# Inverse roots as a power on GpSimd, Silu and Sigmoid by way of Tanh, and one inversion of row sums as a power, in a four-layer image kernel

## The chip, the cores and the metric

The kernel runs on one core of one Trainium2 chip. The metric is the device time of one execution in microseconds (us), lower is better. A core has five engines with a queue each, worked off in order: TensorE (PE in the profile; its weight loads are PEld), VectorE (DVE), ScalarE (ACT), GpSimd (POOL) and SyncE (SP), which here issues the transfers.

## The reference

Eight images of 256 channels and 32 x 32 places, in fp32, go through four layers. Each layer is `x = x + layer(group_norm(x))`, with 32 groups of 8 channels.

```python
# layer 0: attention over the 1024 places, 8 heads of 64, q and k of length 1, scale 10
# layers 1 and 2: 3x3 convolutions, 256 to 256 channels
# layer 3:
xn = layernorm(xs, norm_w, norm_b)                    # over the 256 channels
xm = mamba_v(xc, ...) + skip_scale * xc               # 4 blocks of 64 channels
g  = jax.nn.sigmoid(Q)                                # Q: two small convolutions of xm
# gate, depthwise and 1x1 convolutions -> xm2
x_global = mha(xm2, ...)                              # 8 heads of 32, softmax over 1024 places
x_out = gelu(layernorm(concat([x_local, x_global]) @ fc_w.T + fc_b))
# normalize each channel over its places, 3x3 depthwise, layernorm, 1x1
def mamba(...):                                       # 128 inner channels, 16 states
    u  = silu(conv1d(u)); dt = softplus(...)
    y  = selective_scan(u, dt, B, C, A, D)            # h = exp(dt*A)*h + dt*u*B, over 1024 places
    return y * silu(z) @ outw.T
```

Four kinds of places in it matter here: the inverse square roots of the norms (group norm, layer norm, the length of q and k), the two `silu` of each Mamba block, the `sigmoid` of the gate, and the division by the softmax's row sums in the attention of layer 3.

## The kernel before

Channels lie on the 128 partitions, in two tiles, and places along the free dimension (N = 1024, halves of 512). One image at a time goes through `layer0`, `layer1`, `layer2` and `layer3`; the next image is loaded ahead. The code is written for a framework that sets the waits, and orders the instructions of each engine's queue by its own plan; the order is fixed when the program is built. Working tiles come from one pool of 20 buffers (`work`, tile tag `t`); PSUM has two `mm` tiles of 512 columns, two `big` and one `acc` of 1024.

- `rsqrt_of` (L135): VectorE adds eps (L137), ScalarE takes the square root (L138), VectorE the reciprocal (L139). `group_norm` calls it on a 128x2 tile, four times per image, and the channel norm near the end of layer 3 once. Whatever follows (L168) needs its result.
- `layer_norm` (L177), three times per image: means by a matmul (L185), squares, variances by a matmul (L196) into an 8x128 tile, then add (L204), square root (L205), reciprocal (L206), and a matmul that spreads the result over the partitions (L211).
- `rows_of` in `layer0` (L407): the sum of squares of each row of q and k, square root (L426), maximum with 1e-12 (L427), reciprocal (L428); then the row is scaled (L435, L436).
- `mamba` (L562), four blocks per image. A prologue: a projection, a convolution of four taps on VectorE (L588, L597), Silu on ScalarE (L600), a projection of u (L606) and of dt (L619), softplus from Abs, Exp and Ln (L622 to L629), the product of dt and u (L631). Then a loop over 16 states, with one state spread ahead: a row of B comes by DMA (L638), ScalarE makes exp(dt*A) (L641), TensorE spreads C (L646), GpSimd multiplies (L653), VectorE scans (L662) and multiplies by C (L663), TensorE adds up (L665). Last, u is joined (L672), Silu of z is made from PSUM (L676) and multiplied in on GpSimd (L677), and projected (L680, L683). In VectorE's queue the last seven of the 16 multiplies (L663) stand behind the last scan.
- The gate of layer 3: two matmuls per half (L802, L816), Sigmoid (L824), multiply (L826).
- `attention` (L334) of layer 3: for each pair of heads and half of the places eight units of scores (L344), Exp (L352) and values (L360). The values' matmul gives the row sums too, in the upper 32 rows; `take` copies values (VectorE, L762) and sums (ScalarE, L763) out of PSUM. Four heads fill one tile of sums, `rs[t]`. Then `note` finds its smallest and largest sum (L331, L332), L776 inverts, L777 multiplies, L778 adds a bias:

```python
        for t in range(2):
            r = rs[t][:, 0:N]
            note(r)
            nc.vector.reciprocal(r, r)
            nc.vector.tensor_mul(o[t][:, 0:N], o[t][:, 0:N], r)
```

In VectorE's queue the part for `t = 0` stands between the PSUM copies of the second and the third pair of heads, so in the middle of the attention.

The functions with `exact` belong to a second pass that is taken only if a row sum was out of bounds; with these inputs it isn't taken.

Of the kernel before, what the change touches and what calls it, by code (L numbers as in the profile page):

```python
# [10 lines left out]
F32 = mybir.dt.float32  # L11
# [17 lines left out]
def preact_stack(ctx: ExitStack, tc: tile.TileContext, I, out, cols):  # L29
# [38 lines left out]
    def col(name, i=0, rows=slice(0, P)):  # L68
        at = cols[name] + i
        return vec[rows, at : at + 1]  # L70
# [60 lines left out]
    a_neg = wp.tile([P, NB * DS], F32, name="a_neg")  # L131
    nc.scalar.activation(a_neg, vec[:, cols["alog"] : cols["alog"] + NB * DS], AF.Exp)
    nc.vector.tensor_scalar_mul(a_neg, a_neg, -1.0)

    def rsqrt_of(t, eps):  # L135

        nc.vector.tensor_scalar_add(t, t, eps)  # L137
        nc.scalar.activation(t, t, AF.Sqrt)  # L138
        nc.vector.reciprocal(t, t)  # L139

    def channel_stats(srcs):

# [34 lines left out]
    def layer_norm(srcs, dsts, finish):  # L177

        sq = []
        for t in range(2):  # L180
            sq.append(work("ln_sq"))
        for h in range(2):
            pm = mm_tile()
            for t in range(2):
                nc.tensor.matmul(  # L185
                    pm, mean_w, srcs[t][:, HALVES[h]], start=t == 0, stop=t == 1
                )
            for t in range(2):
                nc.vector.tensor_sub(dsts[t][:, HALVES[h]], srcs[t][:, HALVES[h]], pm)
                nc.scalar.activation(  # L190
                    sq[t][:, HALVES[h]], dsts[t][:, HALVES[h]], AF.Square
                )
        pv = mm_tile()
        for i in range(NKT):
            for t in range(2):
                nc.tensor.matmul(  # L196
                    pv[0:NKT, 0:P],
                    var_w[:, i],
                    sq[t][:, i * P : (i + 1) * P],
                    start=i == 0 and t == 0,  # L200
                    stop=i == NKT - 1 and t == 1,
                )
        rs = sp.tile([NKT, P], F32, tag="ln_rs", name="ln_rs")
        nc.vector.tensor_scalar_add(rs, pv[0:NKT, 0:P], 1e-5)  # L204
        nc.scalar.activation(rs, rs, AF.Sqrt)  # L205
        nc.vector.reciprocal(rs, rs)  # L206
        for h in range(2):
            pr = mm_tile()
            for i in range(4):
                blk = h * 4 + i  # L210
                nc.tensor.matmul(  # L211
                    pr[:, i * P : (i + 1) * P],
                    ident[0:NKT, blk : blk + 1].to_broadcast([NKT, P]),
                    rs,
                    start=True,
                    stop=True,
                )
            for t in range(2):
                part = dsts[t][:, HALVES[h]]
                nc.vector.tensor_mul(part, part, pr)  # L220
                finish(t, part)
# [167 lines left out]
    def layer0(xt, exact=False):  # L389
        xn = [work("xn0"), work("xn1")]  # L390
        group_norm(xt, [t[:, 0:N] for t in xn])

        v = vp.tile([P, NKT, 512], F32, tag="v", name="v")

        def values(kt):
            ps = mm_tile()
            for c in range(2):
                nc.tensor.matmul(
                    ps,
                    xn[c][:, kt * P : (kt + 1) * P],  # L400
                    wqkv[:, c, 1024:1536],
                    start=c == 0,
                    stop=c == 1,
                )
            nc.vector.tensor_copy(v[:, kt], ps)

        def rows_of(first, name):  # L407

            a = work(name)
            ss = sp.tile([P, 2], F32, tag="ss", name="ss", bufs=4)  # L410
            for h in range(2):
                ps = mm_tile()
                for c in range(2):
                    nc.tensor.matmul(  # L414
                        ps,
                        wqkv[:, c, first : first + P],
                        xn[c][:, HALVES[h]],
                        start=c == 0,
                        stop=c == 1,
                    )  # L420
                nc.vector.tensor_copy(a[:, HALVES[h]], ps)
            sq = work("sq")
            nc.scalar.activation(
                sq[:, 0:N], a[:, 0:N], AF.Square, accum_out=ss[:, 0:1]
            )
            nc.scalar.activation(ss[:, 1:2], ss[:, 0:1], AF.Sqrt)  # L426
            nc.vector.tensor_scalar_max(ss[:, 1:2], ss[:, 1:2], 1e-12)  # L427
            nc.vector.reciprocal(ss[:, 1:2], ss[:, 1:2])  # L428
            return a[:, 0:N], ss[:, 1:2]

        qs, ks = [], []
        for t in range(4):
            q, rq = rows_of(t * P, "q")
            k, rk = rows_of(512 + t * P, "k")
            nc.vector.tensor_scalar(q, q, rq, 10.0, ALU.mult, ALU.mult)  # L435
            nc.vector.tensor_scalar_mul(k, k, rk)  # L436
            qs.append(q)
            ks.append(k)
            for kt in (2 * t, 2 * t + 1):
                values(kt)  # L440

        o = []

        def heads():
            for t in range(4):
                o.append(work("o"))
                for e in range(2):
                    yield head(t, e)

        def head(t, e):  # L450
            rows = slice(e * 64, e * 64 + 64)
            at = t * P + e * 64

            def take(half, acc):
                nc.vector.tensor_copy(o[t][rows, half], acc)

            return {
                "q": qs[t][rows],
                "k": ks[t][rows],
                "v": lambda kt: v[:, kt, at : at + 64],  # L460
                "rows": rows,
                "take": take,
            }

        def pair(t):
            ot = work("o")
            o.append(ot)
            rows = [slice(e * 64, e * 64 + 64) for e in range(2)]

            def v_of(e):  # L470
                at = t * P + e * 64
                return lambda kt: v[:, kt, at : at + 64]

            def take(h, acc, total):
                ps = mm_tile()
                for e in range(2):
                    nc.tensor.matmul(
                        ps[rows[e]],
                        ones,
                        total[:, HALVES[e]],  # L480
                        start=True,
                        stop=True,
                    )
                rs = work("rs0")[:, 0:HALF]
                nc.scalar.copy(rs, ps)
                note(rs)
                nc.vector.reciprocal(rs, rs)
                nc.vector.tensor_mul(ot[:, HALVES[h]], acc, rs)

            return {  # L490
                "q": [qs[t][r] for r in rows],
                "k": [ks[t][r] for r in rows],
                "v": [v_of(e) for e in range(2)],
                "take": take,
            }

        if exact:
            attention_exact(heads())
        else:
            attention([pair(t) for t in range(4)], True)  # L500

        def evac(m, half, ps):
            nc.vector.scalar_tensor_tensor(
                xt[:, m, half], ps, col("b_out", m), xt[:, m, half], ALU.add, ALU.add
            )

        project(wout, o, evac)
# [54 lines left out]
    def mamba(i, xn, xm):  # L562
# [33 lines left out]
        for k in range(3):  # L596
            nc.vector.scalar_tensor_tensor(  # L597
                uu, raw[:, k : k + N], col("convw", 4 * i + k), uu, ALU.mult, ALU.add
            )
        nc.scalar.activation(uu, uu, AF.Silu)  # L600


        low = work("low")
# [69 lines left out]
            uu, uu, col("mD", i), y_acc, ALU.mult, ALU.add  # L673
        )
        z = work("z")
        in_proj(P, lambda h, ps: nc.scalar.activation(z[:, HALVES[h]], ps, AF.Silu))  # L676
        nc.gpsimd.tensor_mul(uu, uu, z[:, 0:N])  # L677
        for h in range(2):
            ps = mm_tile()
# [12 lines left out]
    def mixer_attention(x2, exact=False):  # L692
# [80 lines left out]
        for t in range(2):  # L773
            r = rs[t][:, 0:N]
            note(r)
            nc.vector.reciprocal(r, r)  # L776
            nc.vector.tensor_mul(o[t][:, 0:N], o[t][:, 0:N], r)  # L777
            nc.vector.tensor_scalar_add(o[t][:, 0:N], o[t][:, 0:N], col("ain_b", 4 + t))  # L778
        return o

    def layer3(xt, out_b, exact=False):
# [31 lines left out]
        for h in range(2):  # L813
            for j in range(2):
                ps = mm_tile()
                nc.tensor.matmul(  # L816
                    ps,
                    qpr[:, 2 * j : 2 * j + 2].rearrange("q b m -> q (b m)"),
                    q4[0:NB, HALVES[h]],
                    start=True,  # L820
                    stop=True,
                )
                gate = work("gate")[:, 0:HALF]
                nc.scalar.activation(gate, ps, AF.Sigmoid, bias=col("qpwb", j))  # L824
                part = inner(xm[j])[:, HALVES[h]]
                nc.vector.tensor_mul(part, part, gate)  # L826
        xg = xm
# [237 lines left out]
```

## Time and profile before

| | |
|---|---|
| Time, median of 2 runs | 9571.7 us (9569.48 to 9573.92) |
| The profiled execution: its time / its span | 9565.23 us / 9563.5 us |
| PE busy | 7354.8 us, 77% of the span |
| DVE busy | 5074.7 us, 53% |
| ACT busy | 2543.9 us, 27% |
| POOL busy | 2190.2 us, 23% |
| Mean granted TensorE clock | 0.862 |
| HBM read / written | 286.83 MB / 10.49 MB |

The span is the time from the first to the last instruction; the time is that of the whole execution. In the rows of instruction groups the columns are: source line, engine, operation, output<-input with partitions x elements, count, then busy us and mean ns of one, then the engine's idle time just before them and what ended it. In the timeline the columns are: start, length, engine, line, operation, tiles, count, and in brackets the idle time before it with what ended that. A line of the timeline can stand for several instructions in a row. `ACT_TABLE_LOAD` is ScalarE's change to another set of function tables.

### The profile page before, as it was taken

To read this page: it belongs to the slowest core of one execution; us is meant where nothing else is said; L and a number is where in the kernel's file an instruction comes from. 1 tells how busy PE (TensorE), PEld (TensorE's weight loads), DVE (VectorE), ACT (ScalarE), POOL (GpSimd) and SP (SyncE) were. 2 spreads that over 40 slices of the span, in tenths; PEclk is the share of its full clock that TensorE was granted. 3 is DMA by queue.
4 is the path that set the end of the run, shared out by engine and by line. 5 is a ranking of instruction groups with operands and counts; after the bars stand their busy time and mean duration, and the time that the engine had idled before them with its cause. 6 is when DMAs were issued, how large, how long until landed. Compare 5 with 4: busy or idle time off the path is not lost.

```text
span 9563.5 us, 51820 instructions
## 1 busy us (share of the span) xinstructions
PE 7354.8 (77%) x19650; PEld 2690.0 (28%) x19650; DVE 5074.7 (53%) x4146; ACT 2543.9 (27%) x2835; POOL 2190.2 (23%) x1021
## 2 busy tenths in 40 slices
PE   9767897678975789757897578976789757897577
PEld 2322233222332223322233222332223322233222
DVE  6466364663646636466364663646536465364653
ACT  3121331213312133121331213312133121331213
POOL 0253002530025300253002530025300252002520
PEclk9878998788987889878898788987889878898788
DMA  1111001110012100121001210012100121001210
GB/s 51 36 64 42 0 9 36 69 38 2 8 36 69 38 0 9 36 69 38 3 7 36 69 38 5 5 36 71 36 9 0 36 71 36 5 1 36 71 36 5
DMA packets 86139, 300.76 MB, mean 31 GB/s; under 512 B 9844, under 2 KB 12532, under 8 KB 85368
## 3 DMA queue, kind: packets, MB, share of 16 engines
q1 hardware_dynamic: 85880, 297.36, 9.1%
q8 instruction: 156, 2.56, 0.1%
q14 instruction: 103, 0.84, 0.0%
HBM read 286.83 MB, written 10.49 MB: 31 GB/s over the span
## 4 chain that ended last, share of the span: by engine, by line
PE 59%; DVE 23%; issue 9%; POOL 4%; ACT 4%; DMA 0%; DVEq 0%; POOLq 0%; ACTq 0%
PE mm L533 11%; PE mm L360 10%; DVE hs L662 10%; PE big L344 7%; PE acc L665 5%; PE mm L255 4%; PE big L646 4%; PE acc L344 4%; PE mm L414 3%; DVE hs L663 2%; POOL hs L653 2%; DVE u L597 1%; DVE dw L920 1%; PE mm L606 1%; PE mm L716 1%
## 5 line engine op out<-in xcount | busy, mean ns | idle before, releaser
L665 PE MATMUL acc<-hs,ident 128*128 128x512 f32 x2048 | 1211.6, 726 | 1257.2 <-DVE hs L663 1256.9
L653 POOL TENSOR_TENSOR hs<-a,hs 128x1024 f32<-128x1024 f32 x512 | 1887.5, 3715 | 250.5 <-DMA hs<-b_rows 230.2
L662 DVE TENSOR_TENSOR_SCAN hs<-da,hs 128x1024 f32<-128x1024 f32 x512 | 1826.0, 3598 | 219.6 <-POOL hs L653 204.4
L360 PE MATMUL mm<-p,v 128*64 128x512 f32 x4096 | 1098.0, 617 | 0.0
L646 PE MATMUL big<-u,w_mxpw 128*128 128x512 f32 x2048 | 1076.3, 655 | 0.0
L533 PE MATMUL mm<-im,w_wc 128*128 128x512 f32 x2304 | 1033.5, 612 | 29.2 <-DVE im L168 25.6
L641 ACT ACTIVATE da<-dt,a_neg 128x1024 f32<-128x1024 f32 x512 | 563.7, 1142 | 1648.0 <-DVE hs L662 1460.9
L352 ACT ACTIVATE p<-big 128x1024 f32<-128x1024 f32 x688 | 702.4, 1023 | 1014.4 <-PE big L344 1013.4
L665 PEld LDWEIGHTS acc<-hs,ident 128*128 128x128 f32 x2048 | 437.2, 224 | 1894.3 <-DVE hs L663 1447.0
L663 DVE TENSOR_TENSOR hs<-hs,big 128x1024 f32<-128x1024 f32 x512 | 616.8, 1207 | 422.6 <-PE big L646 415.5
L344 PE MATMUL big<-q,k 32*128 32x512 f32 (+1 forms) x2752 | 772.1, 639 | 0.0
L646 PEld LDWEIGHTS big<-u,w_mxpw 128*128 128x128 f32 x2048 | 455.3, 224 | 650.8 <-issue 650.8
L533 PEld LDWEIGHTS mm<-im,w_wc 128*128 128x128 f32 x2304 | 450.4, 196 | 600.4 <-issue 600.4
L762 DVE COPY o<-mm 32x512 f32<-32x512 f32 x128 | 87.6, 684 | 879.6 <-PE mm L360 838.1
L696 POOL MEMSET v<- 128x2048 f32 x8 | 14.4, 1804 | 2195.1 <-PE mm L360 2195.1
L374 DVE TENSOR_TENSOR p<-p 128x1024 f32<-128x1024 f32 x384 | 470.5, 1225 | 42.1 <-ACT p L352 3.0
L628 POOL TENSOR_TENSOR dt<-dt,e 128x1024 f32<-128x1024 f32 x32 | 74.8, 2338 | 1566.5 <-ACT dt L627 1566.5
L360 PEld LDWEIGHTS mm<-p,v 128*64 128x64 f32 x4096 | 205.4, 135 | 770.0 <-issue 655.5
L352 ACT ACTIVATE p<-acc 128x1024 f32<-128x1024 f32 x336 | 344.0, 1024 | 288.5 <-PE acc L344 287.1
L344 PE MATMUL acc<-q,k 64*128 64x512 f32 (+1 forms) x1344 | 377.5, 638 | 0.0
L514 POOL MEMSET dwim<- 128x34 f32 x16 | 2.0, 127 | 1579.2 <-ACT p L352 1557.2
L344 PEld LDWEIGHTS big<-q,k 32*128 32x128 f32 (+1 forms) x2752 | 208.1, 184 | 552.0 <-issue 519.5
(198 smaller groups left out, 6359.7 us busy)
## 6 DMA issues: line engine op xcount, KB each, us to landing
hs<-b_rows SPq DMA_DIRECT2D x512, 512.0 KB, 4.2
xt<-in_x SPq DMA_DIRECT2D x8, 1024.0 KB, 4.8
out<-xt SPq DMA_DIRECT2D x32, 256.0 KB, 2.0
w_wc<-in_wc SPq DMA_DIRECT2D x4, 1152.0 KB, 12.2
b_rows<-low SPq DMA_DIRECT2D x32, 64.0 KB, 1.9
w_wqkv<-in_wqkv SPq DMA_DIRECT2D x2, 768.0 KB, 7.0
w_ainw<-in_ainw SPq DMA_DIRECT2D x2, 384.0 KB, 4.5
w_wout<-in_wout SPq DMA_DIRECT2D x4, 128.0 KB, 7.3
```

What stands on the lines that cost most here:

```text
L255: nc.tensor.matmul(ps, w[:, k, m * P : (m + 1) * P], src[:, HALVES[h]], start=k == 0, stop=k == last,)
L344: nc.tensor.matmul(s[:, HALVES[e]], pair["k"][e][:, kt * P : (kt + 1) * P], pair["q"][e][:, HALVES[h]], start=True, stop=True,)
L352: nc.scalar.activation(p, s, AF.Exp)
L360: nc.tensor.matmul(pair["acc"][e * 64 : e * 64 + 64], pair["v"][e](kt), u["p"][:, HALVES[e]], start=kt == 0, stop=kt == NKT - 1,)
L374: nc.vector.tensor_add(pair["sum"], pair["sum"], u["p"])
L533: nc.tensor.matmul(image(ps), w[:, c, 3 * dy + dx, m * P : (m + 1) * P], im[c][:, 16 * h + dy : 16 * h + dy + 16, dx : dx + 32], start=n == 0,
L641: nc.scalar.activation(da[:, 0:N], dd, AF.Exp, scale=a_neg[:, i * DS + s : i * DS + s + 1])
L646: nc.tensor.matmul(c_all[:, HALVES[h]], mxpw[:, 0, i, at : at + 1].to_broadcast([P, P]), u[:, HALVES[h]], start=True, stop=True,)
L653: nc.gpsimd.tensor_mul(hs[:, 0:N], du[:, 0:N], hs[:, 0:N])
L662: nc.vector.tensor_tensor_scan(hh, da[:, 0:N], hh, 0.0, ALU.mult, ALU.add)
L663: nc.vector.tensor_mul(hh, hh, c_all)
L665: nc.tensor.matmul(y_acc[:, HALVES[h]], ident, hs[:, HALVES[h]], start=s == 0, stop=s == DS - 1,)
```

## The change

Four edits.

1. `rsqrt_of` becomes an addition on VectorE and a power of -0.5 on GpSimd; `layer_norm` copies its variances out of PSUM and calls it. The roots of q and k become a maximum with 1e-24 and the same power.
2. Silu is written with Tanh. For u: Tanh of half on ScalarE, `0.5*t + 0.5` on VectorE, multiply on GpSimd. For z: half of z is copied from PSUM, Tanh, and `(t + 1) * z/2` on VectorE.
3. Sigmoid is written with Tanh, and `0.5*t + 0.5` on VectorE follows.
4. Of the two inversions of row sums in layer 3's attention, that of `t = 0` becomes a power of -1 on GpSimd.

```diff
@@ -131,12 +131,26 @@
     a_neg = wp.tile([P, NB * DS], F32, name="a_neg")
     nc.scalar.activation(a_neg, vec[:, cols["alog"] : cols["alog"] + NB * DS], AF.Exp)
     nc.vector.tensor_scalar_mul(a_neg, a_neg, -1.0)
+    mhalf = wp.tile([P, P], F32, name="mhalf")
+    nc.gpsimd.memset(mhalf, -0.5)
+    minus1 = wp.tile([P, 1], F32, name="minus1")
+    nc.gpsimd.memset(minus1, -1.0)
+    hqpwb = wp.tile([P, 2], F32, name="hqpwb")
+    nc.vector.tensor_scalar_mul(
+        hqpwb, vec[:, cols["qpwb"] : cols["qpwb"] + 2], 0.5
+    )
+
+
+    def silu(dst, src, th):
+
+        nc.scalar.activation(th, src, AF.Tanh, scale=0.5)
+        nc.vector.tensor_scalar(th, th, 0.5, 0.5, ALU.mult, ALU.add)
+        nc.gpsimd.tensor_mul(dst, src, th)
 
     def rsqrt_of(t, eps):
 
         nc.vector.tensor_scalar_add(t, t, eps)
-        nc.scalar.activation(t, t, AF.Sqrt)
-        nc.vector.reciprocal(t, t)
+        nc.gpsimd.tensor_tensor(t, t, mhalf[0:t.shape[0], 0:t.shape[1]], ALU.pow)
 
     def channel_stats(srcs):
 
@@ -201,9 +215,8 @@
                     stop=i == NKT - 1 and t == 1,
                 )
         rs = sp.tile([NKT, P], F32, tag="ln_rs", name="ln_rs")
-        nc.vector.tensor_scalar_add(rs, pv[0:NKT, 0:P], 1e-5)
-        nc.scalar.activation(rs, rs, AF.Sqrt)
-        nc.vector.reciprocal(rs, rs)
+        nc.vector.tensor_copy(rs, pv[0:NKT, 0:P])
+        rsqrt_of(rs, 1e-5)
         for h in range(2):
             pr = mm_tile()
             for i in range(4):
@@ -423,9 +436,8 @@
             nc.scalar.activation(
                 sq[:, 0:N], a[:, 0:N], AF.Square, accum_out=ss[:, 0:1]
             )
-            nc.scalar.activation(ss[:, 1:2], ss[:, 0:1], AF.Sqrt)
-            nc.vector.tensor_scalar_max(ss[:, 1:2], ss[:, 1:2], 1e-12)
-            nc.vector.reciprocal(ss[:, 1:2], ss[:, 1:2])
+            nc.vector.tensor_scalar_max(ss[:, 1:2], ss[:, 0:1], 1e-24)
+            nc.gpsimd.tensor_tensor(ss[:, 1:2], ss[:, 1:2], mhalf[:, 0:1], ALU.pow)
             return a[:, 0:N], ss[:, 1:2]
 
         qs, ks = [], []
@@ -597,7 +609,7 @@
             nc.vector.scalar_tensor_tensor(
                 uu, raw[:, k : k + N], col("convw", 4 * i + k), uu, ALU.mult, ALU.add
             )
-        nc.scalar.activation(uu, uu, AF.Silu)
+        silu(uu, uu, work("th")[:, 0:N])
 
 
         low = work("low")
@@ -673,7 +685,17 @@
             uu, uu, col("mD", i), y_acc, ALU.mult, ALU.add
         )
         z = work("z")
-        in_proj(P, lambda h, ps: nc.scalar.activation(z[:, HALVES[h]], ps, AF.Silu))
+        zh = work("zh")
+        in_proj(
+            P,
+            lambda h, ps: nc.scalar.activation(
+                zh[:, HALVES[h]], ps, AF.Identity, scale=0.5
+            ),
+        )
+        nc.scalar.activation(z[:, 0:N], zh[:, 0:N], AF.Tanh)
+        nc.vector.scalar_tensor_tensor(
+            z[:, 0:N], z[:, 0:N], 1.0, zh[:, 0:N], ALU.add, ALU.mult
+        )
         nc.gpsimd.tensor_mul(uu, uu, z[:, 0:N])
         for h in range(2):
             ps = mm_tile()
@@ -773,7 +795,12 @@
         for t in range(2):
             r = rs[t][:, 0:N]
             note(r)
-            nc.vector.reciprocal(r, r)
+            if t == 0:
+                nc.gpsimd.tensor_tensor(
+                    r, r, minus1.to_broadcast([P, N]), ALU.pow
+                )
+            else:
+                nc.vector.reciprocal(r, r)
             nc.vector.tensor_mul(o[t][:, 0:N], o[t][:, 0:N], r)
             nc.vector.tensor_scalar_add(o[t][:, 0:N], o[t][:, 0:N], col("ain_b", 4 + t))
         return o
@@ -821,7 +848,8 @@
                     stop=True,
                 )
                 gate = work("gate")[:, 0:HALF]
-                nc.scalar.activation(gate, ps, AF.Sigmoid, bias=col("qpwb", j))
+                nc.scalar.activation(gate, ps, AF.Tanh, bias=hqpwb[:, j : j + 1], scale=0.5)
+                nc.vector.tensor_scalar(gate, gate, 0.5, 0.5, ALU.mult, ALU.add)
                 part = inner(xm[j])[:, HALVES[h]]
                 nc.vector.tensor_mul(part, part, gate)
         xg = xm
```

## The prediction

> **What bounds the kernel now.** I read the page first: engine shares, slices, chain. No engine is full; TensorE comes nearest.
>
> ```profile
> PE 7354.8 (77%) x19650; PEld 2690.0 (28%) x19650; DVE 5074.7 (53%) x4146; ACT 2543.9 (27%) x2835; POOL 2190.2 (23%) x1021
> PE   9767897678975789757897578976789757897577
> POOL 0253002530025300253002530025300252002520
> PE 59%; DVE 23%; issue 9%; POOL 4%; ACT 4%; DMA 0%; DVEq 0%; POOLq 0%; ACTq 0%
> ```
>
> The slices repeat eight times, once per image. ScalarE holds 4% of the chain, so most of what is taken off ScalarE was not waited for. Next I read the groups by shape, for prices, and then the timeline of one image (the fourth), for where each edit lies. The prologue of a Mamba block, before its scan loop:
>
> ```profile
> 3965.12 1.06 ACT L600 ACTIVATE u<-u 128x1024 f32<-128x1024 f32 x1 [3.61 <-DVE u L597]
> 3966.23 3.63 PE L606 MATMUL mm<-u,w_mxpw 128*36 128x512 f32 x4 [6.64 <-ACT u L600]
> 3972.65 1.06 ACT L623 ACTIVATE e<-a 128x1024 f32<-128x1024 f32 x1 [2.18 <-DVE a L622]
> 3973.73 1.28 ACT L624 ACT_TABLE_LOAD   x1
> 3975.02 1.06 ACT L624 ACTIVATE e<-e 128x1024 f32<-128x1024 f32 x1
> 3976.11 0.69 DVE L625 TENSOR_SCALAR dt<-e 128x1024 f32<-128x1024 f32 x1 [3.55 <-ACT e L624]
> 3980.57 2.34 POOL L628 TENSOR_TENSOR dt<-dt,e 128x1024 f32<-128x1024 f32 x1 [112.73 <-ACT dt L627]
> ```
>
> Each instruction starts when the one before it ends: this stretch is serial, and every microsecond put in shows 32 times. The end of the scan loop:
>
> ```profile
> 4056.11 2.29 DVE L662 TENSOR_TENSOR_SCAN hs<-da,hs 128x1024 f32<-128x1024 f32 x1 [1.07 <-POOL hs L653]
> 4058.32 2.56 DVE L663 TENSOR_TENSOR hs<-hs,big 128x1024 f32<-128x1024 f32 x2
> 4059.57 1.99 PE L665 MATMUL acc<-hs,ident 128*128 128x512 f32 x4
> ```
>
> The first of the two multiplies ends at 4059.6, and TensorE takes it at 4059.57: VectorE is just in time. Layer norm:
>
> ```profile
> 3951.50 0.28 DVE L204 TENSOR_SCALAR ln_rs<-mm 8x128 f32<-8x128 f32 x1 [2.52 <-PE mm L196]
> 3951.81 0.31 ACT L205 ACTIVATE ln_rs<-ln_rs 8x128 f32<-8x128 f32 x1 [2.17 <-DVE ln_rs L204]
> 3952.15 0.94 DVE L206 RECIPROCAL ln_rs<-ln_rs 8x128 f32<-8x128 f32 x1 [0.38 <-ACT ln_rs L205]
> 3953.14 2.05 PE L211 MATMUL mm<-ln_rs,ident 8*128 8x128 f32 x16 [1.69 <-DVE ln_rs L206]
> ```
>
> Serial too. The mixer's attention, where TensorE is busy without a gap (131.00 of 131.00 us between 4553 and 4684 in the table by windows):
>
> ```profile
> 4624.72 1.21 DVE L332 TENSOR_REDUCE chk<-rs 128x1 f32<-128x1024 f32 x1
> 4625.96 6.55 DVE L776 RECIPROCAL rs<-rs 128x1024 f32<-128x1024 f32 x1
> 4637.14 0.68 DVE L762 COPY o<-mm 32x512 f32<-32x512 f32 x1 [2.58 <-PE mm L360]
> 4637.91 0.58 ACT L763 COPY rs<-mm 32x512 f32<-32x512 f32 x1 [0.76 <-DVE o L762]
> 4638.51 1.02 ACT L352 ACTIVATE p<-big 128x1024 f32<-128x1024 f32 x1
> ```
>
> The first inversion runs in the middle of the attention and ends with 2.58 us to spare, after its multiply and add, before the next PSUM copy. That copy releases a ScalarE copy, which stands ahead of exponentials that TensorE needs.
>
> **What the Trainium skill says.** "ScalarE: Activation LUTs", sections "Table sets: the hidden batching unit" and "What ACT_TABLE_LOAD costs": tanh is in exp's set, sqrt is not, and a load takes 1283 ns plus a drain, 2.66 us together. The trace's loads take 1283 ns, but at L624 only 1.31 us pass from the end of one ACTIVATE to the next: I use 1.29. "GPSIMD Engine Reference", section 3.1: a two-input GpSimd operation takes about 2.6 cycles per element (4497 ns at 2048 elements). The trace agrees: 2338 ns at 1024 and 1264 ns at 512, so 0.19 us plus 2.1 ns per element. The page has no price for pow. It gives a ceiling of about 3 operations per cycle there, and in section 7 four cycles per step of a dependent fp32 chain, at 1.2 GHz. If pow is a logarithm and an exponential of some 45 operations in 20 dependent steps (my assumption), that is an estimate of 15 cycles per element if well overlapped and 80 if not. No run here shows it yet.
>
> **The unknown: pow.** Per element 12.5 to 67 ns; I take the geometric middle, 35 cycles or 29 ns, since nothing favours an end. With the 0.19 us fixed part: 30 us for 128x1024 (13 to 68), 3.9 us for 8x128 (1.8 to 8.7), 0.25 us for 128x2. Below that stands the multiply's own rate (2.34 us), which pow can't beat, having the same operands; above, a routine that isn't vectorized.
>
> **The change part by part**, with the order of the built instructions at hand.
>
> *Table loads.* Of 194 loads in the groups, 80 stay: one at the start, Ln and the Exp behind it in each Mamba block (64), Gelu (8), and an Exp after it (7). Only L624's are on the path, 32 x 1.29 = 41 us. Those at L600, L676, L138, L205 and L352 start while ScalarE waits for others; L641's stays, beneath GpSimd's subtraction.
>
> *Silu of u.* Tanh costs what Silu did (1.06). New: a VectorE tensor_scalar (0.69, L625's row) and a GpSimd multiply (2.34), with gaps of 0.03 and 0.14: 3.20 us before L606 can start. GpSimd's queue is empty there, so the multiply has no company, but nothing covers it. 32 x (3.20 - 1.29) = +61 us, load included.
>
> *Silu of z.* Two scaled copies, Tanh and a VectorE multiply-add of 1.25 us. Tanh waits for a buffer that GpSimd's last multiply frees (4056.1), so it is ready before the last scan ends (4058.4): no stall. But the multiply-add stands on VectorE between that scan and seven queued multiplies, where TensorE is just in time: +1.25, x 32 = +40 us. If TensorE had slack there, 0.
>
> *Sigmoid.* The load at L824 goes (1.28, between L810 and the gate), one 128x512 tensor_scalar of about 0.4 comes in front: -0.9 x 8 = -7 us.
>
> *Layer norm* (24). Before, L204 to L211 is 1.64 us. After: copy 0.28, add 0.18, pow 3.9, gaps 0.22: 4.6. +2.96 x 24 = +71 us (20 to 186).
>
> *Group norm, L2 norms.* A square root of 0.20, a reciprocal of 0.17 and gaps become one 0.25 pow with gaps of 0.17: about 0.42 against 0.44; 0, and up to +20 us over 40 norms if pow has a fixed cost of 0.5. The 64 L2 roots hold VectorE no longer than before, and TensorE's next copies have a microsecond to spare. 0.
>
> *Row sums.* 8 x 6.55 us leave VectorE, but they were hidden: nothing gained. In the built order the multiply of o by rs stands on VectorE ahead of the next pair's PSUM copies. Pow starts at 4626.1; 2.0 us of multiply and add follow it; the copy is due at 4637.14. So 9.0 us are free, and 2.7 more, since the exponential at 4638.5 is needed by TensorE only at about 4642. Beyond 11.7 us TensorE stands still, and having no slack never makes it up: (30 - 11.7) x 8 = +146 us (10 to 454).
>
> Sum: 61 + 40 - 7 + 71 + 0 + 146 = +311 us. The profiled execution took 9565.2 us (span 9563.5), so 9876; the median shown, 9571.7, lies 6.5 above it: 9883 us.
>
> **Rivals.** (A) Pow runs near VectorE's reciprocal rate (6.55 us at 1024). Then the row sums are hidden and the layer norms even: 94 us remain, 9667 us. For it: the vector width is the same; against: two transcendental steps. (B) Pow runs element by element. The same page's section 3.2 has [...]247,699 ns for 2048 elements, 121 ns each: 124 us and 15.7 us, so the row sums cost 898, the layer norms 355: with 94 that is 9571.7 + 1347 = 10919 us. (C) The other side: ScalarE's 114 removed loads all count, and the new VectorE and GpSimd work lies beneath other blocks' work. Place: ScalarE's queue in front of each waiting ACTIVATE; price 114 x 1.28 = 146 us; 9426 us. It decides only if pow stays below 11.7 us and over 79 of the 114 lie on the path (101 us of additions to beat). The timeline shows 32 plus the 8 of the gates.
>
> **How the numbers follow.** Forecast 0.57, A 0.25, B 0.14, C 0.04. A measurement of this kernel tells about 2% (191 us) from no change; by the sums above that is crossed at a pow of 19 us for 1024 elements. Forecast and B are slower, except the forecast's lower end (0.02 to 0.03); A is within 2%; most of C too. Faster 0.03, same 0.27, slower 0.70. The range is the estimate's own ends: 13 us gives +124, 68 us gives +734; with the small unknowns 9680 to 10310.
>
> **What would show it.** The rows of pow at 128x1024, 8x128 and 128x2 decide most. L211's matmuls should wait about 4.6 us after L196; L606's for GpSimd's multiply. A gap of some 18 us in TensorE should stand once per image inside the mixer's attention, with VectorE waiting for GpSimd. 80 loads should remain, 64 of them in Mamba blocks. I am wrong if the 128x1024 pow is below 19 or above 68 us, if the attention keeps no gap though pow is long, or if the blocks grow by other than some 3.2 us each.

## The result, and the profile after

| | before | after |
|---|---|---|
| Time, median | 9571.7 us | 11639.6 us (11628.7 to 11650.5) |
| Ratio | | 1.216, 95% interval 1.211 to 1.221 |
| The profiled execution: its time / its span | 9565.2 / 9563.5 us | 11650.5 / 11648.7 us |
| Mean granted TensorE clock | 0.862 | 0.784 |

The change makes the kernel 22% slower: 2068 us, where 311 were predicted, and beyond the range's upper end of 10310. The direction was right.

The page after: engine shares, three rows of slices, and the chain that ended last by engine and by line.

```profile
PE 7707.4 (66%) x19650; PEld 2776.6 (24%) x19650; DVE 5061.5 (43%) x4131; ACT 2405.0 (21%) x2625; POOL 4149.9 (36%) x1191
PE   9666496664966649666495664956649566495664
POOL 0453304533045330453304533045330453304533
PEclk9778597785977859878597785977859778597785
...
PE 46%; POOL 20%; DVE 19%; issue 10%; ACT 3%; DMA 1%; DVEq 0%; POOLq 0%; ACTq 0%
POOL rs L799 11%; PE mm L545 9%; PE mm L373 8%; DVE hs L674 8%; PE big L357 6%; POOL ln_rs L153 4%; PE mm L268 3%; PE acc L677 3%; PE acc L357 3%; PE big L658 2%; PE mm L427 2%; DVE hs L675 2%; POOL hs L665 2%; DVE u L609 1%; DVE dw L948 1%
```

GpSimd's share of the chain goes from 4% to 20%, and its two largest entries are powers: `rs` at L799 (edit 4) and `ln_rs` at L153 (edit 1, in the layer norms). TensorE executes the same 19650 matmuls and is busy 353 us longer with them: the granted clock has a hole of 5 tenths once per image. The same row of the kernel before has none:

```profile
PEclk9878998788987889878898788987889878898788
```

Waiting alone does not lengthen busy time, so there are two losses, not one.

The powers, in the groups of GpSimd by shape (after the bar: busy us, mean ns of one, idle time before):

```profile
L799 POOL TENSOR_TENSOR rs<-rs,minus 128x1024 f32<-128x1024 f32 x8 | 1305.8, 163226 | 1137.5 <-DVE chk L345 1137.5
L153 POOL TENSOR_TENSOR ln_rs<-ln_rs,mhalf 8x128 f32<-8x128 f32 x24 | 498.4, 20768 | 759.1 <-DVE ln_rs L152 759.1
...
L440 POOL TENSOR_TENSOR ss<-ss,mhalf 128x1 f32<-128x1 f32 x64 | 34.7, 542 | 317.4 <-DVE ss L439 317.4
L153 POOL TENSOR_TENSOR rs<-rs,mhalf 128x2 f32<-128x2 f32 x32 | 22.4, 701 | 853.4 <-DVE rs L152 853.4
```

163.2 us against the 30 assumed, 20.8 against 3.9, 0.70 against 0.25. From 2 to 128 columns (20.77 - 0.70) / 126 = 159 ns per column, from 128 to 1024 (163.23 - 20.77) / 896 = 159 ns again: a power takes 0.38 us plus 159 ns per column.

The attention of layer 3, fourth image, in the timeline (some rows of TensorE, VectorE, ScalarE and GpSimd):

```profile
5431.85 1.13 PE L357 MATMUL big<-q,k 32*128 32x512 f32 x4
5432.90 1.08 PE L373 MATMUL mm<-p,v 128*64 128x512 f32 x4
5433.32 163.23 POOL L799 TENSOR_TENSOR rs<-rs,minus 128x1024 f32<-128x1024 f32 x1 [141.58 <-DVE chk L345]
...
5598.63 0.68 DVE L784 COPY o<-mm 32x512 f32<-32x512 f32 x1
5599.40 0.58 ACT L785 COPY rs<-mm 32x512 f32<-32x512 f32 x1 [155.02 <-DVE o L784]
5601.07 1.97 PE L373 MATMUL mm<-p,v 128*64 128x512 f32 x4 [151.56 <-ACT p L365]
5602.98 2.08 PE L357 MATMUL big<-q,k 32*128 32x512 f32 x4
5604.98 1.98 PE L373 MATMUL mm<-p,v 128*64 128x512 f32 x4
5606.89 2.08 PE L357 MATMUL big<-q,k 32*128 32x512 f32 x4
```

The wait travels as the prediction drew it: the multiply of `o` by the inverted sums stands in VectorE's queue ahead of a PSUM copy (L784), that copy releases a ScalarE copy (L785), behind which stand exponentials, and TensorE waits for one of these: 151.56 us. The prediction's own formula, power minus 11.7 us of slack, gives 163.2 - 11.7 = 151.5. What it did not have is in the rows around the stall: before it, one unit of four score matmuls and four value matmuls takes 2.06 us (5431.85 to 5433.91, the next start); after it, 3.91 us (5602.98 to 5606.89). The table by windows (window, length, busy us of PE, PEld, DVE, ACT and POOL with counts, granted clock) has the same:

```profile
5361.00:5431.00 70.00, 70.00 (x274) 16.95 (x274) 5.67 (x9) 40.21 (x43) 0.00 (x0) 1.00 0.00 0
5431.00:5595.00 164.00, 18.51 (x72) 4.31 (x70) 2.15 (x2) 7.17 (x7) 161.68 (x1) 0.56 0.00 0
5595.00:5655.00 60.00, 53.93 (x112) 11.19 (x112) 5.39 (x7) 18.89 (x21) 1.55 (x1) 0.50 0.00 0
```

Full clock before the stall, half in it, and still half after it, though TensorE is busy again. It stays so to the end of the attention, 79 us later (5601 to 5680); in the eight images it lasts 77 to 79 us.

A layer norm, and the two places of a Mamba block:

```profile
4730.65 0.28 DVE L218 COPY ln_rs<-mm 8x128 f32<-8x128 f32 x1 [2.54 <-PE mm L210]
4730.97 0.21 DVE L152 TENSOR_SCALAR ln_rs<-ln_rs 8x128 f32<-8x128 f32 x1
4731.26 20.77 POOL L153 TENSOR_TENSOR ln_rs<-ln_rs,mhalf 8x128 f32<-8x128 f32 x1 [10.51 <-DVE ln_rs L152]
4752.09 3.77 PE L224 MATMUL mm<-ln_rs,ident 8*128 8x128 f32 x16 [21.47 <-POOL ln_rs L153]
```

```profile
4896.39 1.06 ACT L146 ACTIVATE th<-u 128x1024 f32<-128x1024 f32 x1 [4.91 <-DVE u L609]
4897.48 0.69 DVE L147 TENSOR_SCALAR th<-th 128x1024 f32<-128x1024 f32 x1 [1.12 <-ACT th L146]
4898.25 2.34 POOL L148 TENSOR_TENSOR u<-u,th 128x1024 f32<-128x1024 f32 x1 [11.34 <-DVE th L147]
4900.64 3.63 PE L618 MATMUL mm<-u,w_mxpw 128*36 128x512 f32 x4 [9.79 <-POOL u L148]
...
4987.67 2.29 DVE L674 TENSOR_TENSOR_SCAN hs<-da,hs 128x1024 f32<-128x1024 f32 x1 [1.08 <-POOL hs L665]
4989.88 1.20 DVE L696 SCALAR_TENSOR_TENSOR z<-z,zh 128x1024 f32<-128x1024 f32 x1
4990.99 2.34 DVE L675 TENSOR_TENSOR hs<-hs,big 128x1024 f32<-128x1024 f32 x2
```

The layer norm's serial stretch is 21.44 us (4730.65 to 4752.09) against 1.64 before. The Mamba rows are as predicted: 4.25 us from Tanh to L618 where Silu to L606 took 1.10, and the multiply-add of z (L696) between the last scan and the queued multiplies.

### The profile page after: what moved, and what is told of

Read it like the earlier page. It is cut to its first block, busy times and chain, and to the rows that moved or that the text cites. A ratio compares the mean times of both kernels' runs of the same rounds, so it can differ in the third digit from the quotient of the medians.

```text
span 11648.7 us, 51847 instructions
## 1 busy us (share of the span) xinstructions
PE 7707.4 (66%) x19650; PEld 2776.6 (24%) x19650; DVE 5061.5 (43%) x4131; ACT 2405.0 (21%) x2625; POOL 4149.9 (36%) x1191
## 4 chain that ended last, share of the span: by engine, by line
PE 46%; POOL 20%; DVE 19%; issue 10%; ACT 3%; DMA 1%; DVEq 0%; POOLq 0%; ACTq 0%
POOL rs L799 11%; PE mm L545 9%; PE mm L373 8%; DVE hs L674 8%; PE big L357 6%; POOL ln_rs L153 4%; PE mm L268 3%; PE acc L677 3%; PE acc L357 3%; PE big L658 2%; PE mm L427 2%; DVE hs L675 2%; POOL hs L665 2%; DVE u L609 1%; DVE dw L948 1%
## 5 line engine op out<-in xcount | busy, mean ns | idle before, releaser
L373 PE MATMUL mm<-p,v 128*64 128x512 f32 x4096 | 1247.0, 694 | 1212.5 <-ACT p L365 1212.5
L665 POOL TENSOR_TENSOR hs<-a,hs 128x1024 f32<-128x1024 f32 x512 | 1905.6, 3749 | 239.0 <-DMA hs<-b_rows 219.6
L799 POOL TENSOR_TENSOR rs<-rs,minus 128x1024 f32<-128x1024 f32 x8 | 1305.8, 163226 | 1137.5 <-DVE chk L345 1137.5
L658 PE MATMUL big<-u,w_mxpw 128*128 128x512 f32 x2048 | 1101.7, 668 | 0.0
L365 ACT ACTIVATE p<-big 128x1024 f32<-128x1024 f32 x688 | 702.4, 1023 | 1210.4 <-PE big L357 1208.4
L653 ACT ACTIVATE da<-dt,a_neg 128x1024 f32<-128x1024 f32 x512 | 563.7, 1142 | 1624.5 <-DVE hs L674 1458.6
L357 PE MATMUL big<-q,k 32*128 32x512 f32 (+1 forms) x2752 | 870.7, 714 | 0.0
L153 POOL TENSOR_TENSOR ln_rs<-ln_rs,mhalf 8x128 f32<-8x128 f32 x24 | 498.4, 20768 | 759.1 <-DVE ln_rs L152 759.1
L784 DVE COPY o<-mm 32x512 f32<-32x512 f32 x128 | 87.6, 684 | 1131.9 <-PE mm L373 1090.2
L224 PE MATMUL mm<-ln_rs,ident 8*128 8x128 f32 x384 | 90.6, 426 | 515.2 <-POOL ln_rs L153 515.2
L357 PE MATMUL acc<-q,k 64*128 64x512 f32 (+1 forms) x1344 | 423.0, 709 | 0.0
L699 POOL TENSOR_TENSOR u<-u,z 128x1024 f32<-128x1024 f32 x32 | 74.8, 2338 | 970.2 <-DVE u L684 970.2
```

The lines of the kernel that those rows point to most:

```text
L153: nc.gpsimd.tensor_tensor(t, t, mhalf[0:t.shape[0], 0:t.shape[1]], ALU.pow)
L357: nc.tensor.matmul(s[:, HALVES[e]], pair["k"][e][:, kt * P : (kt + 1) * P], pair["q"][e][:, HALVES[h]], start=True, stop=True,)
L365: nc.scalar.activation(p, s, AF.Exp)
L373: nc.tensor.matmul(pair["acc"][e * 64 : e * 64 + 64], pair["v"][e](kt), u["p"][:, HALVES[e]], start=kt == 0, stop=kt == NKT - 1,)
L653: nc.scalar.activation(da[:, 0:N], dd, AF.Exp, scale=a_neg[:, i * DS + s : i * DS + s + 1])
L658: nc.tensor.matmul(c_all[:, HALVES[h]], mxpw[:, 0, i, at : at + 1].to_broadcast([P, P]), u[:, HALVES[h]], start=True, stop=True,)
```

## The experiments

Theory: the time is lost to a power of 159 ns per column in serial places, and to TensorE's half clock after the stall in the attention. Rivals: the parts of the change make each other worse; the stall alone is the loss and the clock only follows the idle time; the new work around Tanh costs more than its rows. A kernel's time is compared with the kernel before on the same chip: 9565.3 us for the first four below, 9570.3 us for the next four, 9570.5 us for the last.

**Edit 4 alone.** The kernel before with this (the constant `minus1` is left out here and below):

```diff
-            nc.vector.reciprocal(r, r)
+            if t == 0:
+                nc.gpsimd.tensor_tensor(
+                    r, r, minus1.to_broadcast([P, N]), ALU.pow
+                )
+            else:
+                nc.vector.reciprocal(r, r)
```

> The kernel before with edit 4 alone: the row sums of t = 0 are inverted by a power on GpSimd. My prediction's mechanism with the measured power (163.2 us) gives a stall of 163.2 - 11.7 = 151.5 us per image, 8 x 151.5 = 1212, so 10784 us. Theory 1: after the stall TensorE also stays at half clock to the end of this attention, and all of that belongs to edit 4; in the changed kernel the same stretch is 189 us per image longer than before, so 9572 + 8 x 189 = 11086 us. Rival: the half clock comes from the sum of all edits (long idle stretches everywhere), and with edit 4 alone it recovers: 10784 us.

Measured: 11071.7 us, ratio 1.157 (1.155 to 1.160). That is +1506 us, 188.3 per image: the stall of 151.6 and 36.7 more, 294 us over the eight images, that no wait for the power accounts for. Some twenty units at 3.91 us instead of 2.06 make 37. This one small edit makes 73% of the loss, and it does so without the others.

**All but edit 4.** The kernel after with

```diff
-            if t == 0:
-                nc.gpsimd.tensor_tensor(
-                    r, r, minus1.to_broadcast([P, N]), ALU.pow
-                )
-            else:
-                nc.vector.reciprocal(r, r)
+            nc.vector.reciprocal(r, r)
```

> The changed kernel with edit 4 undone (VectorE's reciprocal for both). Theory 1 (edit 4 is worth 189 us per image): 11640 - 1514 = 10126 us, with the mixer's attention back at 2.06 us per unit. Rival (edit 4 is the stall alone): 11640 - 1212 = 10428 us, with the attention still slow.

Measured: 10142.2 us, ratio 1.060 (1.058 to 1.062).

**Tanh alone (edits 2 and 3).** The kernel after with all powers undone, edit 4 as above and

```diff
-        nc.gpsimd.tensor_tensor(t, t, mhalf[0:t.shape[0], 0:t.shape[1]], ALU.pow)
+        nc.scalar.activation(t, t, AF.Sqrt)
+        nc.vector.reciprocal(t, t)
...
-        nc.vector.tensor_copy(rs, pv[0:NKT, 0:P])
-        rsqrt_of(rs, 1e-5)
+        nc.vector.tensor_scalar_add(rs, pv[0:NKT, 0:P], 1e-5)
+        nc.scalar.activation(rs, rs, AF.Sqrt)
+        nc.vector.reciprocal(rs, rs)
...
-            nc.vector.tensor_scalar_max(ss[:, 1:2], ss[:, 0:1], 1e-24)
-            nc.gpsimd.tensor_tensor(ss[:, 1:2], ss[:, 1:2], mhalf[:, 0:1], ALU.pow)
+            nc.scalar.activation(ss[:, 1:2], ss[:, 0:1], AF.Sqrt)
+            nc.vector.tensor_scalar_max(ss[:, 1:2], ss[:, 1:2], 1e-12)
+            nc.vector.reciprocal(ss[:, 1:2], ss[:, 1:2])
```

> The kernel before with edits 2 and 3 alone (Silu and Sigmoid by Tanh), every root and inversion as before. The prediction's terms: +61 for Silu of u, +40 for Silu of z, -7 for Sigmoid: 9572 + 94 = 9666 us. Rival (all removed table loads counted, the new work hidden): below 9572, down to 9480. Rival (the multiply-add of z is hidden): 9626 us.

Measured: 9648.7 us, ratio 1.0086 (1.0069 to 1.0103): +83 us, where the prediction's terms for these edits made +94. The difference to all but edit 4 is edit 1: 10142.2 - 9648.7 = 493 us. The three parts together, 1506 + 493 + 83 = 2082 us, make the measured 2068 to within 14, less than the intervals leave open: edit 4 and the rest add up. Edit 1 was not run alone; its 493 is a difference, and would hide what it and the Tanh edits do to each other.

The single Tanh terms can be read from the traces, since TensorE runs the same matmuls in the same order before and here. Set side by side, the projection of u (L606 before) starts 100 us later in the sum of the 32 blocks, 3.11 each where 3.20 were forecast; 46 us of that come back before the first matmul that adds up (L665), where the load at L624 was to give 41. The scan loops with the blocks' last projections are 36 us longer, where Silu of z was to cost 40; but the loops also shift by up to 17 us in a run below that leaves Silu of z alone. The gate gives nothing, where 7 us were forecast.

**The multiply of `t = 0` moved behind the attention.** Edit 4 alone, and its multiply tied behind the second inversion by a factor of one, so that it no longer stands ahead of the PSUM copies:

```diff
         for t in range(2):
-            r = rs[t][:, 0:N]
-            note(r)
...
+            note(rs[t][:, 0:N])
+        r = rs[0][:, 0:N]
+        nc.gpsimd.tensor_tensor(r, r, minus1.to_broadcast([P, N]), ALU.pow)
+        nc.vector.reciprocal(rs[1][:, 0:N], rs[1][:, 0:N])
+        one = sp.tile([P, 1], F32, tag="one", name="one")
+        nc.vector.tensor_scalar(one, rs[1][:, 0:1], 0.0, 1.0, ALU.mult, ALU.add)
...
+        nc.vector.scalar_tensor_tensor(
+            o[0][:, 0:N], o[0][:, 0:N], one, r, ALU.mult, ALU.mult
+        )
...
```

> Edit 4 alone, but the multiply of o by the inverted sums of t = 0 is tied to the inversion of t = 1, so that on VectorE it stands behind all PSUM copies of the attention. Theory (the loss of edit 4 comes from the place of the waiting multiply in VectorE's queue): the power runs beside the second half of the attention, the attention keeps its 2.06 us per unit, and only what is left of the power after the attention's end stalls, about 4626 + 163 - 4697 = 92 us per image: 9572 + 740 = 10310 us. Rival (a GpSimd power by itself slows TensorE, ScalarE or VectorE beside it, wherever it is waited for): near 11086 us.

Measured: 10313.4 us, ratio 1.078 (1.076 to 1.080). The same eight powers of 163 us cost 748 us instead of 1506: half the loss was the place of one multiply in VectorE's queue. Some 294 of the 758 us saved are the half clock, for the attention runs at full speed to its end. What is left is the power's remainder beyond that end, where TensorE's output projection waits for the multiply (us in total, times, longest); some 100 us of shorter waits in that projection fall away for it.

```profile
PE mm L258 <- DVE o L788: 863.2, 8, 109.0
```

**A power that fits the slack, and one that just does not.** Edit 4 for the first 64 or 128 of the 1024 columns, the others inverted on VectorE as before (the diff is that of 128):

```diff
-            nc.vector.reciprocal(r, r)
+            if t == 0:
+                nc.gpsimd.tensor_tensor(
+                    r[:, 0:128], r[:, 0:128], minus1.to_broadcast([P, 128]), ALU.pow
+                )
+                nc.vector.reciprocal(r[:, 128:N], r[:, 128:N])
+            else:
+                nc.vector.reciprocal(r, r)
```

64 columns:

> The kernel before, but 64 of the 1024 columns of row sums of t = 0 are inverted by the power on GpSimd and 960 by VectorE's reciprocal. By the measured rows the power takes 0.38 + 64 x 0.159 = 10.6 us, below the 11.7 us that the prediction counted as free. Theory (11.7 us are free): no change, 9565 us. Rival (any waiting multiply in that place starts the half clock): 8 x 38 = 304 more, 9870 us.

128 columns:

> As the one with 64 columns, but 128 columns by the power: 0.38 + 128 x 0.159 = 20.7 us, 9 us over the 11.7 that are free. Theory 1 (a stall of 9 us is long enough to put TensorE on half clock, and narrow matmuls don't bring it back): 8 x (9 + 38) = 376 more, 9941 us. Theory 2 (only a long stall does that): 8 x 9 = 72 more, 9637 us.

Measured: 9573.6 us with 64 (ratio 1.0003, 0.9995 to 1.0012) and 9926.9 us with 128 (1.037, 1.036 to 1.039). The power and the wait for it, groups and waits of the run with 128:

```profile
L780 POOL TENSOR_TENSOR rs<-rs,minus 128x128 f32<-128x128 f32 x8 | 165.8, 20728 | 1137.8 <-DVE chk L335 1137.8
```

```profile
DVE o L786 <- POOL rs L780: 121.2, 8, 15.2
```

10.5 us of power are free, as 11.7 us of slack say. 20.7 us overrun the slack by 9.0, which would be 72 us over eight images; 357 were lost. The other 285, or 36 per image, are the 36.7 that the full power lost beside its stall: a stall of nine microseconds costs the clock as much as one of 151. The trace has it: TensorE's first row after the stall in the fourth image, and the window behind it, busy without a gap at a clock of 0.50. In the eight images the half clock lasts 77 to 80 us.

```profile
4783.92 1.98 PE L363 MATMUL mm<-p,v 128*64 128x512 f32 x4 [9.07 <-ACT p L355]
4784.00:4858.00 74.00, 74.00 (x152) 15.13 (x152) 2.74 (x4) 23.16 (x25) 0.34 (x4) 0.50 0.00 0
```

The row of L780 is also the price of the power at 128 partitions: 20.73 us, against 20.77 at 8 partitions and another exponent.

**Full-size matmuls after the stall.** Edit 4 alone, and six multiplications by the 128x128 identity in TensorE's queue, behind the fourth unit of the third pair's second half, which is shortly after the stall. One column of the result is copied by VectorE to a tile that nothing reads.

```diff
+            if dense and pair is pairs[2] and h == 1 and kt == 3:
+                dense()
...
+        def dense():
+            d = mm_tile()
+            for n in range(6):
+                nc.tensor.matmul(
+                    d, ident, qk[0][:, 0:HALF], start=n == 0, stop=n == 5
+                )
...
```

> Edit 4 alone, and six extra 128x128x512 matmuls, whose result is thrown away, stand in TensorE's queue behind the fourth unit of the pair and half in which the stall lies. Theory 1 (the half clock lasts because the attention's matmuls use 32 rows or 64 columns of the array; full ones end it): about 20 units per image go back from 3.91 to 2.06 us, less some 7.5 us for the extra matmuls: 11072 - 8 x (37 - 7.5) = 10836 us. Rival (the clock stays low for a time, or for the rest of the stage, whatever runs): the extra matmuls add 8 x 10.3 us: 11154 us.

Measured: 10864.5 us, ratio 1.135 (1.133 to 1.137): 207 us less than edit 4 alone, by adding work (212 when each is set against the kernel before on its own chip). TensorE's rows around them in the fourth image:

```profile
5278.81 1.97 PE L363 MATMUL mm<-p,v 128*64 128x512 f32 x4 [151.56 <-ACT p L355]
5280.71 2.08 PE L347 MATMUL big<-q,k 32*128 32x512 f32 x4
5282.72 1.98 PE L363 MATMUL mm<-p,v 128*64 128x512 f32 x4
5284.63 6.99 PE L780 MATMUL mm<-q,ident 128*128 128x512 f32 x12
5291.55 1.13 PE L347 MATMUL big<-q,k 32*128 32x512 f32 x4
5292.60 1.08 PE L363 MATMUL mm<-p,v 128*64 128x512 f32 x4
```

The stall is the same 151.56 us. The six (two records each) come a unit and a half after the stall. The units before them run at half clock, those after at full. The granted clock changes 3.0 to 3.4 us after the first of the six has begun, in all eight images, so the last of them run at full clock already. The count closes: of 36.7 us per image 212 / 8 = 26.5 are gone, and the 10.2 left are near the 9.8 that the rows give, 7.0 for the six and one and a half units at 1.85 too much. So the half clock is a loss of its own, and the rival, that it only accompanies the idle time, falls.

Full size is not what it takes, though. The attention ends with twelve value matmuls in a row, with no score matmul between them. In the fourth image of edit 4 alone (a row of TensorE, then a window):

```profile
5434.19 4.20 PE L363 MATMUL mm<-p,v 128*64 128x512 f32 x12
5437.10:5438.30 1.20, 1.20 (x6) 0.14 (x2) 0.00 (x0) 0.00 (x0) 0.00 (x0) 1.00 0.00 0
```

The clock is back before the next 128x128 matmul starts at 5438.32. It is so in all sixteen images of edit 4 alone and of the kernel after, 2.5 to 5.1 us after the first of the twelve. So 64 columns alone do not keep the clock down; it stays down while score matmuls of 32 rows stand between. Whether these alone would do it, or only the alternation, was not run.

**Two kernels out of the table loads.** The prediction found two kinds of exposed loads, Exp's in each Mamba block (L624) and the gate's (L824). A load can be called up earlier, while ScalarE waits for others, with a one-column function of the same set. In the kernel before, none of the four edits made:

```diff
         nc.scalar.activation(uu, uu, AF.Silu)
+        tiny = sp.tile([P, 1], F32, tag="tiny", name="tiny")
+        nc.scalar.activation(tiny, uu[:, 0:1], AF.Exp)
```

> The kernel before, with one more ScalarE instruction in each Mamba block: an Exp of one column behind Silu of u, so that exp's tables are loaded while ScalarE waits for TensorE, not between Abs and Exp. Theory (of all the loads that the change removed, those 32 are what the path saw): 32 x 1.29 = 41 less, 9524 us. Rival (no load is on the path): 9565 us, or a few more.

Measured: 9506.1 us, ratio 0.9933 (0.9920 to 0.9947): below both kernels. ScalarE's rows in the second block of the fourth image:

```profile
4076.07 1.06 ACT L625 ACTIVATE e<-a 128x1024 f32<-128x1024 f32 x1 [3.91 <-DVE a L624]
4077.16 1.06 ACT L626 ACTIVATE e<-e 128x1024 f32<-128x1024 f32 x1
4078.23 1.28 ACT L629 ACT_TABLE_LOAD   x1
```

The load between Abs and Exp is gone from there; there are as many loads as before. Measured from Silu to softplus, the 32 prologues are 41.2 us shorter in sum, 1.25 to 1.29 each but for the first, as expected. The gain is 64; another 17 us lie in the scan loops, half a microsecond each in the mean with both signs, and the reason for those and for the last 6 is open. Between the kernel before and edit 4 alone, which leaves them as they were, the loops differ by 8 us in sum.

And the gate's load too:

```diff
+        tiny = sp.tile([P, 1], F32, tag="tiny", name="tiny")
+        nc.scalar.activation(tiny, xm[1][:, 1:2], AF.Sigmoid)
         q4 = work("q4")
```

> The kernel before with a one-column Exp right after the Silu of u in each Mamba block, as in the run with the early Exp, and now a one-column Sigmoid ahead of the copies of q4, in front of the gate of layer 3. Theory: in the kernel before, two of ScalarE's table loads lie on the path, the one of Exp in each block (32 x 1.29 = 41 us, plus the 17 us by which the scan loops were seen to be shorter with it) and the one of the gate (8 x 1.28 = 10 us). The second now falls while ScalarE waits for the end of the last block, so the time should be about 10 us below that of the early Exp alone: 9496 us, against 9570 before, which is a ratio of 0.992. Rival: ScalarE waits before the gate for something else anyway, so that load was hidden too; the time stays at 9506 us. The difference is near what five rounds can tell, so the rows around the gate in the trace decide: from the second copy of q4 to the first of the gate's functions there should be no load, and the gate's first function should start about 1.3 us sooner after the copy.

Measured: 9502.3 us, ratio 0.9932 (0.9918 to 0.9945). The rows say that the load was on the path: from the start of the second copy of q4 to the end of the last Sigmoid 4.56 us (4464.65 to 4469.21), where the kernel before took 6.13 (4494.90 to 4501.03), so 8 x 1.57 = 12.6 us less there.

```profile
4459.50 0.68 ACT L814 ACTIVATE q<-mm,qdwb 4x512 f32<-4x512 f32 x1 [6.86 <-PE mm L806]
4464.65 0.68 ACT L814 ACTIVATE q<-mm,qdwb 4x512 f32<-4x512 f32 x1 [4.47 <-PE mm L806]
4465.71 0.69 ACT L828 ACTIVATE gate<-mm,vec 128x512 f32<-128x512 f32 x1 [0.37 <-PE mm L820]
...
4468.52 0.69 ACT L828 ACTIVATE gate<-mm,vec 128x512 f32<-128x512 f32 x1 [0.23 <-PE mm L820]
```

The time does not: 4 us less than with the early Exp alone, and the intervals cover each other. Matmul by matmul against the trace with the early Exp alone, the gate's are 10 us closer together and those of the scan loops 11 us further apart. Nothing in the loops was changed, so that looks like their scatter, which is not shown.

## Why the prediction was wrong, step by step

| Step | predicted, us | measured, us | by |
|---|---|---|---|
| Silu of u, Silu of z, Sigmoid | +61, +40, -7 | +83 together | Tanh alone |
| Layer norm, group norm, L2 norms | +71, 0, 0 | +493 together | all but edit 4, less Tanh alone |
| Row sums | +146 | +1506 | edit 4 alone |

**The price of pow failed first.** The step "the geometric middle, 35 cycles or 29 ns, since nothing favours an end" was off by 5.5: 159 ns. The measured value lies outside both bounds, since both, 15 and 80 cycles, came from one assumption, a logarithm and an exponential of some 45 vectorized operations. The case above them, "a routine that isn't vectorized", was named, priced at 121 ns, and then given 0.14 and kept out of the range. It was the nearest of the four and still 24% below the measurement; and it was near by luck, since the figure in the skill ("GPSIMD Engine Reference", section 3.2) is that of a reduction across partitions, another operation. Two estimates of the same unknown, 29 and 121 ns, without a row of the operation in any trace, are not a middle and an outlier but two ends.

**A term was missing.** Put the measured price into the prediction's own sum: the layer norms make 24 x (21.44 - 1.64) = 475, the group norms about 40 x 0.34 = 14 (L152 to the end of the power 0.95 us, where L137 to the end of L139 was 0.61), the row sums 8 x 151.5 = 1212, with 94 for Tanh. That is 1795, and 9565 + 1795 = 11360 against the profiled 11650.5. What is short, 290 us, is the half clock after the stall, 8 x 36.7 = 294. The prediction treated a wait as so many microseconds of wait and the matmuls behind it as unchanged. The skill would have given the first half of this mechanism: "TensorE: Matmul & The Clock Gate", Part 1, has the clock halved after an idle window of about 3.4 us, and here it falls 2.2 to 3.7 us into the stalls of 9 and 151 us. But the page restores it after about as long a busy window, which would make an estimate of 1.7 us per stall (half of 3.4), not 37. The six full-size matmuls (3.0 to 3.4 us) agree with that, and the twelve value matmuls (2.5 to 5.1 us) nearly; 77 us of score and value matmuls in turn do not, and the measurement decides. Rival B, with a price nearer to the truth, did not have this term either: with 159 ns it too would have ended at 11360.

**What held.** The 11.7 us of free time for the row sums: 64 columns cost nothing and the stall is 151.56. The path from the multiply through the PSUM copies to TensorE: moving the multiply took away half the loss. The layer norm as a serial place, where the power's whole length shows. The Tanh terms in sum, 94 against 83 with an interval of 66 to 98. The table loads that stay: 32 at L639, 32 at L653, 8 at L238, 7 at L365 and one at L132, so 80. And that L624's load was exposed: the early Exp took it out with the 41 us that were named. That the other loads but the gate's are hidden is read from the rows and not tried one by one. Rival C, with all 114 on the path, falls with Tanh alone, which takes 80 loads away and is 83 us slower; its bar was also set too low, since the "101 us of additions to beat" are 61 + 40, from which L624's 41 us had already been taken, and the whole additions, some 145 us (32 x 3.20 + 40 + 3), need practically all of the 114. Rival A, a cheap power, falls with the first row of the groups. Of the prediction's own tests one failed at once, "above 68 us".

**What stays open.** Edit 1's parts sum to 489 against the 493 measured, but that leaves out the 16 spreading matmuls of each layer norm, which take 3.77 us after the power and took 2.05 before: 24 x 1.7 = 41 us. Matmul by matmul, the trace of all but edit 4 has 475 us more than that of Tanh alone ahead of the spreading matmuls, 37 in them and 10 behind the group norms, 521 together, where the whole is 491. The 30 us that come back lie in many places, none with more than 6. The square root's removed table loads are not seen among them: eight exposed ones would be 10 us in one place. What gives the 30 back is open, and so is why a power costs 159 ns per column.

## What to carry to other kernels

An operation without a row in any trace and without a price in the notes wants a range from the cheapest to the slowest way in which it could be carried out, and a place in the program where its full length can be hidden; before it is put into the middle of a saturated stage, its length is compared with the slack there (here 11.7 us), and the instructions behind its consumer on the same queue are counted. A stall in front of matmuls with few rows can cost more than its length: look at the granted clock after the stall, and not only at the wait. Loads of function tables that lie on the path are called up early by a one-column function while ScalarE waits, with nothing else moved; that gave 0.7% here, where Silu and Sigmoid by Tanh, which remove 80 of the loads, lost 0.9%.

## What the runs showed of the hardware that was not expected

- Pow on GpSimd costs 0.38 us plus 159 ns per column, whatever the partitions (8x128: 20.77 us, 128x128: 20.73 us), and those two differ in the exponent as well (-0.5 and -1). A multiply of the same 128x1024 tile takes 2.34 us there, and VectorE's reciprocal 6.55.
- After a stall of 9 us or of 151 us, TensorE ran score matmuls of 32 rows and value matmuls of 64 columns in turn at half clock (a unit in 3.91 us instead of 2.06) almost to the end of the attention, 77 to 80 us in both cases. Six 128x128 multiplications by 512 columns brought the full clock back 3.0 to 3.4 us after the first of them began, and the same small matmuls then kept it. Twelve value matmuls without scores between them brought it back too, in 2.5 to 5.1 us. Score matmuls alone were not run.
